# A two-layer graph attention kernel: a new order for the work ahead of the first period

## The chip, the cores and the metric

The kernel runs on one core of a Trainium2 chip. The metric is device time in microseconds (us). Before the change it was 3665.32 us, the median of three runs (3664.4 to 3667.73). The profiled execution took 3661.67 us and its trace spans 3659.8 us.

## What is computed

The input is 64 graphs of 256 nodes with 512 features, and a boolean 256 x 256 matrix for each graph. Two attention layers follow, each on the normalized and rectified input, each added to its input. Cut to what matters:

```python
# layer 0
h = max(layernorm(x), 0)
m = h @ map_w.T + map_b                       # 512 x 512
n = m / norm(m, per head of 64)               # "lengths", 8 heads
cos_adj = (n @ n.T > 0.1), where adj keeps it
q = m @ q_w.T + q_b;  k = m @ k_w.T + k_b     # 512 x 512 each
p = softmax(q @ k.T / 8, masked) * keep
sem = h @ gcn_map_w.T + gcn_map_b             # messages
out = relu((cos_adj * p) @ sem @ gcn_W.T / (sum(cos_adj * p) + 1))
x = x + out
# layer 1: q, k, v from 512 to 256 (4 heads), softmax under the adjacency, Wo
x = x + softmax(q1 @ k1.T / 8, masked) @ v1 @ Wo + bo
```

`gcn_W` is applied to the messages ahead of time: the kernel computes the folded weight `wc` from `gcn_map_w` and `gcn_W`, and the folded bias `bc`, once at the start.

## The kernel before

**Products.** Each 512 x 512 product on 256 nodes is done with seven half-size products in place of eight (`seven_products`, L260). For this each weight is held as seven blocks: four are loaded (`load_seven`, L72), and three are differences that VectorE computes with four subtractions of 128 x 512 (`finish_seven`, L85). The left factor, too, needs four sums, which GpSimd computes (`left_factors`, L250; the tile is `sh` for the normalized input and `sm` for the mapped one). A call of `seven_products` is a Python generator. At each `next` it issues one piece: p24 (two products into one bank, with biases added by ScalarE into u2 and u4), then z and p53 (u5), then a second product added into z, then a third one. Between the pieces VectorE reads z and writes a quarter of the result (L301) or the helper sum uup (L321). The next product into the same bank waits for that read. So TensorE, though it runs alone, hangs on VectorE at the last two pieces of each product.

**Order.** The whole schedule is written out by hand (`tc.manual_schedule()`). Every engine works through its instructions in the order in which the Python code issues them. An engine never overtakes: what stands behind a waiting instruction waits, too. Buffers are handed on in a ring[...], and waits follow from the data.

**Periods.** `period(i)` works on graph i in layer 0, on graph i - 1 in layer 1, and prepares graph i + 1 and graph i + 2. It is called 65 times and takes 56 us each time in the steady state. It begins with the score products `sc` (L401).

**The opening.** Ahead of the first period, the code at L712 to L761 has to bring graph 0 to where a period expects it, and graph 1 half way. It loads everything (L714 to L720), normalizes graph 0 (`normal`, then `normal_input`: transposes `p_t` on TensorE and `sh`), and prepares its edge mask. Then come, in this order:

- the differences of `wm` and the mapped input `mT` (`mapped`, tile `p_m`), with the fold of `wc` (`fold`, L120: 16 products, L127, evictions by ScalarE, L144) between its second and third piece,
- the differences of `wq`, the left factor `sm` and the squares, then the differences of `wk`,
- the first piece of the queries, the squared lengths (`norms`, L358, and `lengths`, L365), the folded bias (`fold_bias`, L131: VectorE spreads `gb` over `gbb`, TensorE multiplies, VectorE copies the bank into `bc`), and the differences of `wc`,
- the rest of queries and keys in turn,
- square root and reciprocal of the lengths (L749, L750) and their spread through DRAM (`spread`), edges and normalization of graph 1 (`normal(1)`), and a load of ScalarE's exp table ahead of its use (L755),
- the messages `p_s` of graph 0 (five pieces), and then graph 1's transposes and its `sh`.

**Loads.** Weights go through the SyncE queue one after the other (L82, L118, L184). The six small loads (`gt`, twice, `gb` and three biases, L44, L46, L95) go through ScalarE's queue. The biases are loaded as 128 x 4 single elements, and so make 512 packets of four bytes each. A completion semaphore is shared by every eighth of these loads, and the issue of a load waits until the load eight places before it has landed.

Of the kernel before, what the change touches and what calls it, by code (L numbers as in the profile page):

```python
# [8 lines left out]
F32 = mybir.dt.float32  # L9
# [20 lines left out]
class Weights:  # L30
# [4 lines left out]
    def __init__(self, nc, const, a):  # L35
        P, D, DH = 128, a["x"].shape[2], 64
        self.nc, self.const, self.a = nc, const, a
        self.ident = const.tile([P, P], F32, name="ident")
        make_identity(nc, self.ident)

        self.gt = const.tile([P, P], F32, name="gt")
        nc.vector.memset(self.gt, 0.0)
        for j in range(2):
            nc.scalar.dma_start(out=self.gt[j * DH:(j + 1) * DH, j * DH:(j + 1) * DH], in_=a["gcn_WT"])  # L44
        self.gb = const.tile([P, D // P], F32, name="gb")
        nc.scalar.dma_start(out=self.gb, in_=a["gcn_map_b"].rearrange("(c p) -> p c", p=P))  # L46
        self.ident_b = const.tile([P, P], BF16, name="ident_b")
        nc.vector.tensor_copy(self.ident_b, self.ident)
        self.below = const.tile([P, 1], F32, name="below")
        nc.vector.memset(self.below, -THRESHOLD)  # L50
        self.ones = const.tile([P, DH], F32, name="ones")
        nc.vector.memset(self.ones, 1.0)

        self.blk32 = const.tile([P, 32], F32, name="blk32")
        nc.vector.memset(self.blk32, 0.0)
        for j in range(2):
            nc.vector.memset(self.blk32[j * DH:(j + 1) * DH, j * 16:(j + 1) * 16], 1.0)

        self.two = const.tile([P, 2, 32], F32, name="two")
        nc.vector.memset(self.two, 0.0)  # L60
        for n in range(2):
            nc.vector.memset(self.two[:, n, n:n + 1], 1.0)
        self.wc = const.tile([P, 7, D // P // 2, D // 2], F32, name="wc")
        self.bc = const.tile([P, D], F32, name="bc")
# [4 lines left out]
        self.nc.sync.dma_start(out=t, in_=ap.rearrange("(c p) f -> p c f", p=128))  # L69
        return t  # L70

    def load_seven(self, keys, name):  # L72

        aps = [self.a[k] for k in (keys if isinstance(keys, tuple) else (keys, keys))]
        half = aps[0].shape[0] // 2
        t = self.const.tile([128, 7, half // 128, half], F32, name=name)
        for n, (i, j) in enumerate(self.BLOCKS):
            f = 0 if isinstance(keys, tuple) else j * half  # L80
            block = aps[j][i * half:(i + 1) * half, f:f + half]
            self.nc.sync.dma_start(out=t[:, n], in_=block.rearrange("(c p) f -> p c f", p=128))  # L82
        return t

    def finish_seven(self, t):  # L85
# [6 lines left out]
    def load_b(self, key, name):  # L92
        ap = self.a[key]
        t = self.const.tile([128, ap.shape[0] // 128], F32, name=name)
        self.nc.scalar.dma_start(out=t, in_=ap.rearrange("(c p) -> p c", p=128))  # L95
        return t

    def load_map(self):
        self.wm, self.bm = self.load_seven("map_wT", "wm"), self.load_b("map_b", "bm")

    def load_scores(self):
        self.wq, self.bq = self.load_seven("q_wT", "wq"), self.load_b("q_b", "bq")
# [14 lines left out]
        for k, t in enumerate(gws):  # L117
            self.nc.sync.dma_start(out=t, in_=gw[:, 2 * k:2 * k + 2, :])  # L118

    def fold(self, gws, bank, put):  # L120

        nc, P = self.nc, 128
        NKC = self.gb.shape[1]
        for c in range(NKC):
            p = bank(f"p_wc{c}", [P, NKC * P])
            for k in range(NKC):
                nc.tensor.matmul(p[:, k * P:(k + 1) * P], gws[k // 2][:, k % 2, c * P:(c + 1) * P], self.gt,  # L127
                                 start=True, stop=True)
            put(c, p)

    def fold_bias(self, gbb, bank):  # L131
        nc, P = self.nc, 128
        NKC = self.gb.shape[1]
        nc.vector.tensor_copy(gbb, self.gb[:, :, None].to_broadcast([P, NKC, P]))
        p = bank("p_bc", [P, NKC * P])
        for k in range(NKC):
            nc.tensor.matmul(p[:, k * P:(k + 1) * P], gbb[:, k, :], self.gt, start=True, stop=True)
        nc.vector.tensor_copy(self.bc, p)

    def put_seven(self, c, p):  # L140
        i, k = divmod(c, self.wc.shape[2])
# [6 lines left out]
def fast_path(ctx, tc, a, w, chk, out):  # L148
# [4 lines left out]
    nc = tc.nc  # L153
    x, adj = a["x"], a["adj"]
    B, S, D = x.shape
    P, DH = 128, 64
    H0, NKC = D // DH, D // P
# [6 lines left out]
    sb2 = ctx.enter_context(tc.tile_pool(name="sb2", bufs=2))  # L164
# [9 lines left out]
    def bank(name, shape=(P, 2, S), dtype=F32):  # L174
        return ring.tile(list(shape), dtype, tag="bank", name=name)
# [23 lines left out]
    def deviations(g):  # L199
        nc.scalar.activation(g.rs, g.rs, AF.Sqrt)  # L200
        nc.vector.reciprocal(g.rs, g.rs)
# [139 lines left out]
    def mapped(g):  # L341
        g.mT = sb1.tile([P, NKC, S], F32, tag="mT", name=f"mT{g.i}")
        return seven_products(g.left_h, w.wm, w.bm, g.mT, f"p_m{g.i}")
# [7 lines left out]
    def halved(g):  # L351
        g.left_m = left_factors(g.mT, "sm", g.i)
# [5 lines left out]
    def norms(g):  # L358

        p = bank(f"p_n{g.i}", [P, S])  # L360
        for c in range(NKC):
            nc.tensor.matmul(p[32 * c:32 * (c + 1), :], w.blk32, g.sq[:, c, :], start=True, stop=True)
        return p

    def lengths(g, p):  # L365
        g.rn = sb1.tile([P, S], F32, tag="rn", name=f"rn{g.i}")
        nc.vector.tensor_scalar_max(g.rn, p, COS_EPS * COS_EPS)
# [9 lines left out]
    def spread(g):  # L377

        g.nT = sb1.tile([P, NKC, S], F32, tag="nT", name=f"nT{g.i}")
        by_head(g.rn, 16, g.nT, f"rn{g.i}")  # L380
# [326 lines left out]
    def normal_input(g):  # L707
        g.hT = turned(g, f"0_{g.i}", "hT")
        g.left_h = left_factors(g.hT, "sh", g.i)

    with tc.manual_schedule():
        spare = small.tile([P, 2], F32, tag="spare", name="spare", bufs=1)  # L712
        nc.vector.memset(spare, 0.0)
        graphs = {0: load(0)}  # L714
        w.load_map()
        gws = [sb2.tile([P, 2, D], F32, tag="e", name=f"gw{k}", bufs=6) for k in range(2)]
        w.load_folded(gws)
        w.load_scores()
        graphs.update({n: load(n) for n in range(1, min(3, B))})
        w.load_rest()  # L720

        def normal(n):
            moments(graphs[n], f"0_{n}")
            deviations(graphs[n])
            normalized(graphs[n], f"0_{n}")

        g = graphs[0]
        normal(0)
        normal_input(g)
        edges(g)  # L730
        w.finish_seven(w.wm)
        m = mapped(g)
        next(m)
        next(m)
        w.fold(gws, bank, w.put_seven)
        next(m)
        w.finish_seven(w.wq)
        next(m)
        halved(g)
        squares(g)  # L740
        w.finish_seven(w.wk)
        q, k, s = queries(g), keys(g), messages(g)
        next(q)
        lengths(g, norms(g))
        w.fold_bias(sb2.tile([P, NKC, P], F32, tag="xn", name="gbb"), bank)
        w.finish_seven(w.wc)
        for step in (k, q, k, q, k, q, k):
            next(step)
        nc.scalar.activation(g.rn, g.rn, AF.Sqrt)  # L749
        nc.vector.reciprocal(g.rn, g.rn)  # L750
        spread(g)
        if B > 1:
            edges(graphs[1])
            normal(1)
        nc.scalar.activation(spare[:, 1:], spare[:, :1], AF.Exp)  # L755
        for _ in range(5):
            next(s)
        if B > 1:
            normal_input(graphs[1])
        if B > 2:  # L760
            moments(graphs[2], "0_2")  # L761
        for i in range(B + 1):
            period(i)
# [3 lines left out]
def general_path(ctx, tc, a, w, out):  # L767

    nc = tc.nc
    x, adj = a["x"], a["adj"]  # L770
    B, S, D = x.shape
    P, DH = 128, 64
    H0, NKC = D // DH, D // P
# [8 lines left out]
    wm = one.tile([P, NKC, D], F32, tag="gwm", name="gwm")  # L782
    nc.sync.dma_start(out=wm, in_=a["map_wT"].rearrange("(c p) f -> p c f", p=P))
    wc = one.tile([P, NKC, D], F32, tag="gwc", name="gwc")
    gws = [one.tile([P, 2, D], F32, tag=f"ggw{k}", name=f"ggw{k}") for k in range(2)]
# [20 lines left out]
    def bank(name, shape):  # L806
        return ps1.tile(shape, F32, tag="gbank", name=name)
# [71 lines left out]
                                     start=(k == 0), stop=(k == NT - 1))  # L879
        return av  # L880

    w.fold(gws, bank, lambda c, p: nc.vector.tensor_copy(wc[:, c, :], p))

    with tc.For_i(0, B) as b:
        xs = one.tile([P, NT, D], F32, tag="gxs", name="gxs")
# [11 lines left out]
        hT = norm_relu_T(xs, "0")  # L897
        mT = one.tile([P, NKC, S], F32, tag="gmT", name="gmT")
        nT = one.tile([P, NKC, S], F32, tag="gnT", name="gnT")
        for m in range(NKC):  # L900
            p = features_first(wm, hT, m, f"gp_m{m}")
# [3 lines left out]
        for t in range(NT):  # L905
            p = tokens_first(wc, hT, t, f"gp_s{t}")
            nc.vector.tensor_add(sem[:, t, :, :DH], p.rearrange("p (h d) -> p h d", d=DH),
                                 w.bc.rearrange("p (h d) -> p h d", d=DH))
        for m in range(NKC):
            sq = two.tile([P, S], F32, tag="gsq", name=f"gsq{m}")  # L910
            nc.gpsimd.tensor_mul(sq, mT[:, m, :], mT[:, m, :])
            p = bank(f"gp_n{m}", [P, S])
# [8 lines left out]
        for m in range(NKC):  # L921
            p = features_first(wq, mT, m, f"gp_q{m}")
            nc.scalar.activation(qT[:, m, :], p, AF.Identity, bias=w.bq[:, m:m + 1])
            p = features_first(wk, mT, m, f"gp_k{m}")
            nc.vector.tensor_scalar_add(kT[:, m, :], p, w.bk[:, m:m + 1])

        for t in range(NT):
            for g in range(H0 // 4):
                name = f"0_{t}_{g}"
# [21 lines left out]
        hT = norm_relu_T(xs, "1")  # L951
# [9 lines left out]
        for t in range(NT):  # L961
            p = tokens_first(w.wv1, hT, t, f"gp_v{t}")
            nc.scalar.copy(v[:, t, :, :DH], p.rearrange("p (h d) -> p h d", d=DH))
        for t in range(NT):
            name = f"1_{t}"
# [7 lines left out]
            p = bank(f"gp_oT{name}", [P, NIC, P])  # L973
# [4 lines left out]
            p = bank(f"gp_o{name}", [P, D])  # L978
# [83 lines left out]
```

## Time and profile before

| What | Value |
|---|---|
| Time, median of three | 3665.32 us |
| Span of the trace | 3659.8 us |
| TensorE (PE) busy | 3614.9 us, 99% |
| VectorE (DVE) busy | 2681.6 us, 73% |
| GpSimd (POOL) busy | 2226.7 us, 61% |
| ScalarE (ACT) busy | 1904.1 us, 52% |
| First transpose on TensorE | 7.90 us after the span's start |
| First score product `sc` | 55.73 us |
| One steady period | 56 us |

The times in the trace count from the span's start. A busy share is an average over the whole execution. The change touches only the first 56 us, which are 1.5% of the span, so the averages say nothing of it. What is needed is the order of instructions on each engine inside this stretch, who ends each idle time of TensorE, and the clock that TensorE was granted there. In a line of a stretch the columns are: from and to, length, busy time (and count of instructions) of PE, PEld (weight loads), DVE, ACT and POOL, granted clock, DMA share, GB/s. In a line of the timeline they are: start, time, engine, line, operation, output and input with shapes, count, and in brackets the idle time before it and what ended it. In a line of waits they are: who waited for whom, total us, number of times, longest.

### The profile page before, as it was taken

The numbers are of one execution on the slowest core, as the hardware profiler recorded it, in microseconds if no ns is written. First come the engines' busy times: TensorE is split into PE (matmuls) and PEld (weight loads), VectorE is DVE, ScalarE is ACT, GpSimd is POOL, SyncE is SP. The second block draws the span as 40 slices with busy tenths as digits, with TensorE's granted clock in tenths as the row PEclk, the third lists the DMA queues.
The fourth block names the chain that finished last, engine by engine and source line by source line (L and its number), as shares of the span: only waits on it lengthen the run. The fifth ranks groups of instructions, "written<-read, shape, count | busy, mean of one in ns | idle before, by whom it ended". The sixth has DMA issues, their size and how long they took to land.

```text
span 3659.8 us, 76416 instructions
## 1 busy us (share of the span) xinstructions
PE 3614.9 (99%) x29153; PEld 3088.7 (84%) x29153; DVE 2681.6 (73%) x5288; ACT 1904.1 (52%) x4480; POOL 2226.7 (61%) x2044
## 2 busy tenths in 40 slices
PE   7999999999999999999999999999999999999997
PEld 6888888888888888888888888888888888888885
DVE  6777777777777777777777777777777777777775
ACT  3455555555555555555555555555555555555543
POOL 3666566566665665666666656656666566566662
PEclk9999999999999999999999999999999999999999
DMA  3121211211211112112112111221121111211211
GB/s 110 46 57 45 56 45 53 60 44 54 58 45 55 51 50 58 44 55 60 43 53 57 47 55 45 53 60 44 53 58 45 55 51 50 58 44 55 60 30 35
DMA packets 361009, 191.73 MB, mean 52 GB/s; under 512 B 272449, under 2 KB 326977, under 8 KB 360641
## 3 DMA queue, kind: packets, MB, share of 16 engines
q1 hardware_dynamic: 358368, 186.76, 18.8%
q8 instruction: 233, 3.82, 0.4%
q14 instruction: 136, 1.11, 0.1%
q10 hardware_dynamic: 2272, 0.04, 0.0%
HBM read 94.67 MB, written 34.34 MB: 35 GB/s over the span
## 4 chain that ended last, share of the span: by engine, by line
PE 97%; DVE 1%; DMA 1%; POOL 0%; issue 0%; ACT 0%; SPq 0%; DVEq 0%; ACTq 0%; POOLq 0%
PE sc L401 9%; PE av L428 9%; PE p_m L276 6%; PE p_k L276 6%; PE p_q L276 6%; PE p_qk L276 6%; PE p_o L553 6%; PE p_v L520 6%; PE p_s L271 6%; PE co L438 5%; PE p_qk_z L276 5%; PE p_k_z L276 5%; PE p_q_z L276 5%; PE p_m_z L276 5%; PE p_s_z L271 4%; PE sm L481 2%
## 5 line engine op out<-in xcount | busy, mean ns | idle before, releaser
L421 POOL TENSOR_TENSOR d<-e 128x512 f32<-128x512 f32 x382 | 595.5, 1585 | 365.5 <-DVE e L417 364.2
L408 ACT ACTIVATE e<-sc 128x512 f32<-128x512 f32 x768 | 383.3, 648 | 382.7 <-PE sc L401 376.4
L465 POOL TENSOR_TENSOR d<-d,e 128x512 f32<-128x512 f32 x252 | 322.9, 1291 | 171.1 <-DVE e L463 171.1
L506 POOL TENSOR_TENSOR xs<-xs,o 128x512 f32<-128x512 f32 x128 | 188.4, 1495 | 341.6 <-DVE o L504 341.6
L254 POOL TENSOR_TENSOR sh<-hT 128x256 f32<-128x256 f32 x128 | 93.2, 728 | 492.6 <-ACT hT L217 315.7
L417 DVE TENSOR_TENSOR e<-e,mask 128x1024 f32<-128x1024 f32 x256 | 379.8, 1504 | 1.2 <-ACT e L408 1.2
L451 DVE SCALAR_TENSOR_TENSOR e<-co,e 128x256 f32<-128x256 f32 (+1 forms) x1024 | 288.0, 346 | 64.5 <-ACT up L448 35.4
L458 POOL TENSOR_TENSOR d<-d,e 128x512 f32<-128x512 f32 x252 | 312.4, 1270 | 0.0
L448 ACT ACTIVATE up<-co,below 128x128 bf16<-128x128 f32 x512 | 160.4, 364 | 185.9 <-PE co L438 180.4
L553 PE MATMUL p_o<-wo,own 128*128 128x512 f32 x512 | 233.7, 600 | 9.6 <-DVE own L548 9.6
L520 PE MATMUL p_v<-wv,hT 128*128 128x256 f32 x1024 | 242.2, 380 | 0.0
L428 PE MATMUL av<-e,sem 128*64 128x256 f32 x2048 | 232.4, 379 | 1.2 <-DVE e L463 1.2
L401 PE MATMUL sc<-qT,kT 64*128 64x256 f32 x2048 | 232.2, 377 | 0.0
L401 PEld LDWEIGHTS sc<-qT,kT 64*128 64x128 f32 x2048 | 198.6, 188 | 23.0 <-ACT hT L217 0.3
L491 DVE RECIPROCAL r<-rt 128x16 f32<-128x16 f32 x64 | 16.5, 258 | 269.1 <-PE rt L489 269.1
L428 PEld LDWEIGHTS av<-e,sem 128*64 128x64 f32 x2048 | 146.6, 137 | 76.3 <-DVE e L463 2.1
L520 PEld LDWEIGHTS p_v<-wv,hT 128*128 128x128 f32 x1024 | 185.0, 191 | 20.1 <-issue 0.3
L231 ACT ACTIVATE xn<-xs,shift,rs 128x512 f32<-128x512 f32 x124 | 100.5, 811 | 192.8 <-POOL d L458 190.3
L194 DVE BATCH_NORM_STATS2 st<-xs 128x6 f32<-128x512 f32 x256 | 173.9, 679 | 25.1 <-POOL xs L506 22.0
L463 DVE SCALAR_TENSOR_TENSOR e<-far,e 128x256 f32<-128x256 bf16 x256 | 189.8, 761 | 0.0
L438 PE MATMUL co<-nT 64*128 64x256 f32 (+1 forms) x2048 | 186.6, 332 | 2.8 <-ACT e L408 2.8
L438 PEld LDWEIGHTS co<-nT 64*128 64x128 f32 x2048 | 163.2, 189 | 21.9 <-ACT e L408 3.1
(198 smaller groups left out, 9279.3 us busy)
## 6 DMA issues: line engine op xcount, KB each, us to landing
xs<-in_x_dram SPq DMA_DIRECT2D x64, 512.0 KB
nT<-by_rn SPq DMA_DIRECT2D x128, 256.0 KB
out_dram<-xs SPq DMA_DIRECT2D x63, 512.0 KB
own<-by_rz SPq DMA_DIRECT2D x128, 128.0 KB
ad<-in_adj_dram SPq DMA_DIRECT2D x64, 64.0 KB
far<-up SPq DMA_TRANSPOSE x256
turn<-flat SPq DMA_TRANSPOSE x248
mask<-adb SPq DMA_TRANSPOSE x128
```

Source lines behind the costliest of these rows:

```text
L271: nc.tensor.matmul(region, src[:, c, :], wt[:, block, c, :], start=p not in opened, stop=True, skip_group_check=True)
L276: nc.tensor.matmul(region[:, f, :], wt[:, block, c, f * P:(f + 1) * P], src[:, c, :], start=p not in opened, stop=True, skip_group_check=True)
L401: nc.tensor.matmul(ps[s][:, j, :], rows[h, c, j * P:(j + 1) * P], cols[h, c, :], start=True, stop=True)
L408: nc.scalar.activation(e[:, s, :], p.rearrange("p j q -> p (j q)"), AF.Exp, scale=SCALE)
L417: nc.vector.tensor_mul(e, e, m)
L421: nc.gpsimd.tensor_add(d, e[:, :, :S], e[:, :, S:])
L428: nc.tensor.matmul(av[s * DH:(s + 1) * DH, n, :], vs[:, j, (h0 + s) * DH:(h0 + s + 1) * DH], q[:, s, j * S:(j + 1) * S], start=(j == 0), s ...
L438: nc.tensor.matmul(ps[s][:, j, j * P:], g.nT[h, c, j * P:(j + 1) * P], g.nT[h, c, j * P:], start=(j == 0), stop=True, skip_group_check=True)
L458: nc.gpsimd.tensor_add(g.d[c], g.d[c], g.e[c][:, :, :S])
L465: nc.gpsimd.tensor_add(g.d[c], g.d[c], g.e[c][:, :, S:])
L520: nc.tensor.matmul(g.p_v[:, t, :], g.h1T[:, c, t * P:(t + 1) * P], w.wv1[:, c, :], start=(c == 0), stop=(c == NKC - 1))
L553: nc.tensor.matmul(p, b.avs1[:, c, t * P:(t + 1) * P], w.wo1[:, c, :], start=(c == 0), stop=(c == NIC - 1))
```

## The change

The opening is put in another order, so that VectorE's work for the weights stands where VectorE was idle, and its work for the lengths and for graph 1 stands beside TensorE's queries and keys. In detail:

- The differences of `wq` follow the first piece of the mapped input, those of `wk` the second, both ahead of the sums that read z.
- The fold of `wc` is split: columns 0 and 1 after the first piece of the mapped input, columns 2 and 3 after the third.
- The spread of the bias, `gbb`, is an operation of its own, right behind the differences of `wm`. The product `p_bc` follows the mapped input directly, and ScalarE, not VectorE, copies it to `bc`.
- The differences of `wc` precede the queries.
- The lengths follow the first pieces of both queries and keys. Square root, reciprocal and spread, and graph 1's edges and normalization, come right behind it and after the queries' second piece, instead of behind all queries and keys. The exp table is loaded there as well.
- Graph 1's transposes precede the last piece of the messages; its `sh` follows it.
- The blocks of `wm` alternate between the SyncE and the ScalarE queue. The six small loads move to GpSimd's queue.

No computation is added or left out.

```diff
-            nc.scalar.dma_start(out=self.gt[j * DH:(j + 1) * DH, j * DH:(j + 1) * DH], in_=a["gcn_WT"])
+            nc.gpsimd.dma_start(out=self.gt[j * DH:(j + 1) * DH, j * DH:(j + 1) * DH], in_=a["gcn_WT"])
...
-        nc.scalar.dma_start(out=self.gb, in_=a["gcn_map_b"].rearrange("(c p) -> p c", p=P))
+        nc.gpsimd.dma_start(out=self.gb, in_=a["gcn_map_b"].rearrange("(c p) -> p c", p=P))
...
-            self.nc.sync.dma_start(out=t[:, n], in_=block.rearrange("(c p) f -> p c f", p=128))
+            queue = (self.nc.sync, self.nc.scalar)[n % queues]
+            queue.dma_start(out=t[:, n], in_=block.rearrange("(c p) f -> p c f", p=128))
...
-        self.nc.scalar.dma_start(out=t, in_=ap.rearrange("(c p) -> p c", p=128))
+        self.nc.gpsimd.dma_start(out=t, in_=ap.rearrange("(c p) -> p c", p=128))
...
-        self.wm, self.bm = self.load_seven("map_wT", "wm"), self.load_b("map_b", "bm")
+        self.wm, self.bm = self.load_seven("map_wT", "wm", 2), self.load_b("map_b", "bm")
...
-    def fold(self, gws, bank, put):
+    def fold(self, gws, bank, put, cs):
...
-        for c in range(NKC):
+        for c in cs:
...
+    def spread_bias(self, gbb):
+        self.nc.vector.tensor_copy(gbb, self.gb[:, :, None].to_broadcast([128, self.gb.shape[1], 128]))
+
     def fold_bias(self, gbb, bank):
...
-        nc.vector.tensor_copy(gbb, self.gb[:, :, None].to_broadcast([P, NKC, P]))
...
-        nc.vector.tensor_copy(self.bc, p)
+        nc.scalar.copy(self.bc, p)
...
         w.finish_seven(w.wm)
+        gbb = sb2.tile([P, NKC, P], F32, tag="xn", name="gbb")
+        w.spread_bias(gbb)
+
         m = mapped(g)
         next(m)
+        w.fold(gws, bank, w.put_seven, (0, 1))
+        w.finish_seven(w.wq)
         next(m)
-        w.fold(gws, bank, w.put_seven)
+        w.finish_seven(w.wk)
         next(m)
-        w.finish_seven(w.wq)
+        w.fold(gws, bank, w.put_seven, (2, 3))
         next(m)
         halved(g)
         squares(g)
-        w.finish_seven(w.wk)
+        w.fold_bias(gbb, bank)
+        w.finish_seven(w.wc)
         q, k, s = queries(g), keys(g), messages(g)
         next(q)
+        next(k)
         lengths(g, norms(g))
-        w.fold_bias(sb2.tile([P, NKC, P], F32, tag="xn", name="gbb"), bank)
-        w.finish_seven(w.wc)
-        for step in (k, q, k, q, k, q, k):
-            next(step)
         nc.scalar.activation(g.rn, g.rn, AF.Sqrt)
         nc.vector.reciprocal(g.rn, g.rn)
         spread(g)
+        next(q)
         if B > 1:
             edges(graphs[1])
             normal(1)
         nc.scalar.activation(spare[:, 1:], spare[:, :1], AF.Exp)
-        for _ in range(5):
-            next(s)
+        for step in (k, q, k, q, k, s, s, s, s):
+            next(step)
         if B > 1:
-            normal_input(graphs[1])
+            graphs[1].hT = turned(graphs[1], "0_1", "hT")
+        next(s)
+        if B > 1:
+            graphs[1].left_h = left_factors(graphs[1].hT, "sh", 1)
```

More of the change, by code (lines that the diff above doesn't have):

```diff
@@ L70, in load_w, with load_seven @@
         return t
-    def load_seven(self, keys, name):
+    def load_seven(self, keys, name, queues=1):
         aps = [self.a[k] for k in (keys if isinstance(keys, tuple) else (keys, keys))]
@@ L880, in mix @@
         return av
-    w.fold(gws, bank, lambda c, p: nc.vector.tensor_copy(wc[:, c, :], p))
+    w.fold(gws, bank, lambda c, p: nc.vector.tensor_copy(wc[:, c, :], p), range(NKC))
     with tc.For_i(0, B) as b:
```

## The prediction

> **What bounds the kernel now.** I read the page first, then stage totals, then TensorE's waits, then VectorE's order, then the granted clock.
>
> ```profile
> span 3659.8 us, 76416 instructions
> ...
> PE 3614.9 (99%) x29153; PEld 3088.7 (84%) x29153; DVE 2681.6 (73%) x5288; ACT 1904.1 (52%) x4480; POOL 2226.7 (61%) x2044
> ...
> PE   7999999999999999999999999999999999999997
> ```
>
> TensorE is busy in all slices but the first and the last. The edit touches only what comes before the first period, so stages tell what there is to gain:
>
> ```profile
> 7.90:55.73 47.83, 38.21 (x261) 33.92 (x262) 28.87 (x56) 12.72 (x35) 9.80 (x12) 0.94 0.54 163
> ...
> 110.00:166.00 56.00, 56.00 (x455) 47.95 (x455) 41.38 (x83) 29.81 (x70) 34.86 (x33) 1.00 0.19 52
> ```
>
> Columns: stretch, length, busy PE, PEld, DVE, ACT, POOL, granted clock, DMA share, GB/s. A steady period has no TensorE idle. The opening, from TensorE's first transpose (7.90) to its first score product `sc` (55.73), has 47.83 - 38.21 = 9.62 us idle, at a mean clock of 0.94. Who ends that idle time:
>
> ```profile
> PE p_bc L137 <- DVE gbb L134: 3.1, 1, 3.1
> PE p_s_z L271 <- DVE sem L301: 2.4, 1, 2.4
> PE p_q L276 <- DVE mT L301: 1.5, 1, 1.5
> PE p_m L276 <- DVE wm L90: 1.4, 1, 1.4
> PE p_m_z L276 <- DVE uup_m L321: 0.6, 1, 0.6
> PE p_s_z L271 <- DVE uup_s L321: 0.5, 1, 0.5
> ```
>
> Every gap is a wait for VectorE, whose order of work is at fault, not its speed:
>
> ```profile
> 21.57 0.42 DVE L321 TENSOR_TENSOR uup_m<-p_m_z,u5p_m 128x256 f32<-128x256 f32 x1 [5.83 <-PE p_m_z L276]
> ...
> 28.79 1.09 DVE L90 TENSOR_TENSOR wk<-wk 128x512 f32<-128x512 f32 x1
> 29.81 0.41 DVE L367 TENSOR_SCALAR rn<-p_n 128x256 f32<-128x256 f32 x1
> 30.14 0.61 DVE L134 COPY gbb<-gb 128x512 f32<-128x512 f32 x1
> ```
>
> VectorE idles 5.83 us, then does the wq and wk differences while TensorE waits. Last, the clock:
>
> ```profile
> 47.00:49.00 2.00, 0.15 (x1) 0.00 (x0) 1.69 (x6) 1.69 (x3) 0.00 (x0) 1.00 0.16 24
> ...
> 50.00:51.00 1.00, 1.00 (x4) 0.67 (x2) 0.00 (x0) 0.00 (x0) 0.00 (x0) 0.50 1.07 210
> ...
> 56.00:57.00 1.00, 1.00 (x8) 0.86 (x10) 0.93 (x3) 0.43 (x1) 0.49 (x1) 0.71 0.00 0
> ```
>
> After the 2.42 us gap the clock is 0.50 until some 56.5. Two groups of `p_s_z` take 1.93 and 2.08 us there against 1.03 at 72.66, and eight transposes 1.91 against 1.04 for eight at 90.50: 0.90 + 1.05 + 0.87 = 2.8 us. So the gap costs more than its length.
>
> **What the Trainium skill says.** "TensorE: Matmul & The Clock Gate", Part 1, says that an idle window of about 3.4 us halves the clock and that the windows run freely. The trace agrees in kind: halved after 2.42 us of idle at 47.15 and again after 2.23 us at 95.11, but not after 3.15 us at 27.75, so where the gap falls matters. "SBUF — State Buffer", Who interferes with whom, says that a VectorE operation with two SBUF inputs contends with GpSimd. It does: a 128x512 difference takes 0.69 us alone, 1.10 beside GpSimd's sums (`wk`, L88 to L90). "DMA: Bandwidth & Descriptors", Issuing engines are not separate DMA queues, says that a second issuing engine saves issue time only; and its SWDGE section, that GpSimd writes its own descriptors, with some 1 us to the first byte. No run here shows a GpSimd load.
>
> **The change part by part.** Times are after the edit unless marked. A product of seven runs as p24, z, p53, z(s2), z(s3); before each z(s..) TensorE waits until VectorE has read z for the last time.
>
> *Loads.* The wm blocks leave at once on two queues; before, the fourth issue ended at 6.66 because it waited for the gt load (4.41 us in the chain of waits). Against this, two blocks (0.5 MB) now run beside graph 0's input. Delay of that input: none if they fill idle DMA time (share 0.81 in the first 10 us), 0.52 MB / 361 GB/s = 1.45 us if they go wholly ahead. I take 0.6: first transpose 8.5, xn ready at 8.8. wm's differences then no longer wait 1.01 us for a load: 0.69 + 0.22 (ident_b, now second) + 2 x 0.69 + 1.10 = 3.4, end 12.2, against 13.03. TensorE's cold start ends at the same place, so its 1.4 us wait nearly goes.
>
> *Six small loads on GpSimd.* Price unknown: lower bound the skill's 1 us each, done by about 7.3; upper bound by the nearest row, queue q10, 0.1% x 16 x 3659.8 / 2272 packets = 26 ns each as rounded, 11.6 ns with 1.5% of the first 110 us: 2048 four-byte packets x 11.6 = 24 us. I take 1 to 2.5 us each[...]. GpSimd's queue holds sh behind them (10.55 before, 11.1 now); p53 needs its last sum only at about 16.8 and sh takes 2.9 to 3.7 us, so up to some 12 us for the six is hidden. gt is due at 13.2, bm at 13.2; both fit.
>
> *Middle of the mapping.* TensorE: p_m second half 12.25 to 13.15; half the fold (3.58 / 2 = 1.79) to 14.95 (gw had landed at 12.77); z 0.89, p53 1.79 to 17.65. VectorE: gbb 0.61 (hidden: wq has not landed), wq's four from about 15.0 to 17.8, mT 18.2; so z(s2) waits 0.6: 18.25 to 19.2. Second half of the fold to 21.0. wk landed at 18.75 in the chain; I keep that: four x 0.69 to 21.5, uup 21.9. So the last z waits 0.95: 21.95 to 22.95, and mT is whole at 23.8 instead of 25.89. Gain 2.1. GpSimd is idle here, hence 0.69.
>
> *After mT.* p_bc follows at once (gbb is long ready), 0.93 to 23.9; p_q 1.8, p_k 1.79, p_n 0.55, q z 0.89: q53 begins at 28.9 instead of 34.54. Gain so far 5.6; the 3.15 and 1.52 us gaps are in it. sm on GpSimd needs 4.5 us as before (beside wc's differences, 0.69 + 3 x 1.10), ready at 28.3, just in time. bc on ScalarE (0.65) is hidden: nobody needs it before the messages.
>
> *Lengths and graph 1's norm under queries and keys.* VectorE after wc (27.8): rn 28.4, sqrt on ScalarE 28.85, reciprocal 1.74 to 30.6, q's first sum 31.0, moments 1.9, sqrt and reciprocal 0.5, xn 1.0 to 34.5, k's first sum 34.9. Behind it waits k's z(s2), which TensorE reaches at 34.3: a new gap of 0.65. The exp table load (1.28) on ScalarE ends at 34.5 ahead of u5 for the keys, needed at 35.8: hidden.
>
> *Messages.* VectorE now holds only their own sums, so the 2.42 us gap goes, and with it the halved clock; graph 1's transposes fill the 0.5 us gap. From q53 to `sc`: 4.47 + 0.89 + 0.65 + 2.73 (three z) + 4.32 (p_s, z, p_s53) + 0.88 + 0.95 + 0.88 = 15.8, with starts 16.1, against 21.19 before. `sc` starts at 45.0 instead of 55.73: **10.7 us gained**. sh for graph 1 comes after the last product, done some 4 us after `sc` begins, and is needed 7.7 us after (63.43 - 55.73). moments(2) ends 1 to 2 us later against `sc`; the masks had 1.15 us of wait, and PE there a queue of scores. Hidden. From `sc` on everything moves as a block: 3665.3 - 10.7 = 3654.6.
>
> **Rivals.** (1) *Timed runs lack the halved clock*, as windows run freely: the gain is 10.7 - 2.8 = 7.9, 3657.4. For: no halving after the 3.15 us gap. Against: half clock three times near the end too, so gaps of this size do hit. (2) *Loads late*: GpSimd's issues at 11.6 ns a packet, 24 us from 1.3, hold sh until 25.3, done 28.2; p53's half 0.9, z 0.95, fold 1.8, z 0.95 and the last sums 0.85 bring mT whole at 33.7 instead of 23.8. Of 10.7 remain 0.8: 3664.5. At 18 us in all mT is whole at 27.7 and 6.8 remain: 3658.5. For: the price is unseen. Against: some 12 us of room. (3) *Slower*: descriptors at twice that, 48 us: sh done at 52.2, mT whole at 57.7, 31.8 after before's 25.89; 10.7 - 2.1 = 8.6 is won later, so 3665.3 + 23.2 = 3688.5. Only the unseen price speaks for it.
>
> **Chances.** Main case 0.62 (3654.6, within 3651 and 3658: input delay 0 to 1.45, wk up to 0.6 us earlier, and one more or less halved window, 3.4 us at half speed = 1.7), rival 1 0.14, rival 2 0.19, rival 3 0.05. Low end 3650.0: mildest bounds (1.2 us) and two halved windows fewer (3.4). High end 3661.5: the middle of rival 2's two sizes. Faster needs under 3658.0: most of the main case, two thirds of rival 1, and a third of rival 2: 0.75; same 0.20; slower 0.05.
>
> **What would show it.** `sc` starting near 45; `p_bc` and `p_s_z` with no wait; clock 1.00 from 12 us to `sc`; TensorE idle in the opening about 2.5 us; wk's differences at 0.69; a steady period still 56.0 us. Wrong if sh starts after 13 (GpSimd's loads), if the first transpose is later than 9.3 (input crowded), or if VectorE waits on wq or wk past 19.

## The result, and the profile after

After takes **3650.43 us** (median of six runs, 3649.96 to 3652.85), before 3664.75 us (six runs, 3663.11 to 3667.73): ratio **0.9961, 95% interval 0.9948 to 0.9974**. That is 14.3 us gained, where 10.7 were forecast.

The page of after, its busy times and TensorE's row of slices, looks as before: only the first slice differs at all.

```profile
span 3651.0 us, 76421 instructions
...
PE 3613.9 (99%) x29153; PEld 3088.9 (85%) x29153; DVE 2680.1 (73%) x5287; ACT 1902.7 (52%) x4481; POOL 2229.8 (61%) x2050
...
PE   8999999999999999999999999999999999999997
```

The work is the same (TensorE 3613.9 against 3614.9 us busy), and a stage shows what the slices can't. Stage totals of after, first transpose to first `sc`, and a steady period:

```profile
8.30:44.41 36.11, 35.27 (x261) 32.81 (x261) 26.77 (x50) 13.55 (x37) 9.52 (x12) 1.00 0.71 205
97.00:153.00 56.00, 56.00 (x456) 47.95 (x455) 41.46 (x82) 29.79 (x70) 34.97 (x32) 1.00 0.17 47
```

The opening has 36.11 - 35.27 = 0.84 us of TensorE idle, in place of 9.62, at a mean clock of 1.00, in place of 0.94. The period is 56.00 us still. What is left of TensorE's waits from 7 to 46 us, after the wait for the first input:

```profile
PE p_m L279 <- DVE wm L91: 0.4, 1, 0.4
PE p_k_z L279 <- DVE kT L304: 0.2, 1, 0.2
PE p_m_z L279 <- DVE uup_m L324: 0.2, 1, 0.2
```

The waits for `gbb`, for `mT` ahead of the queries, and for graph 0's sums are gone. VectorE's order of time in after shows by what:

```profile
15.35 0.69 DVE L88 TENSOR_TENSOR wq<-wq 128x512 f32<-128x512 f32 x1 [2.06 <-DMA wq<-in_L_gnn_q_w_dram]
...
18.14 0.42 DVE L304 TENSOR_TENSOR mT<-p_m_z,u2p_m 128x256 f32<-128x256 f32 x1
18.47 0.68 DVE L88 TENSOR_TENSOR wk<-wk 128x512 f32<-128x512 f32 x1
...
21.25 0.42 DVE L324 TENSOR_TENSOR uup_m<-p_m_z,u5p_m 128x256 f32<-128x256 f32 x1
```

The bracket is VectorE's own idle time and its cause. It waits for data now (the load of `wq`), and both sets of differences are done before the mapping's last sums of `mT`. In before the differences of `wq` stood directly ahead of these last sums:

```profile
24.53 0.69 DVE L90 TENSOR_TENSOR wq<-wq 128x512 f32<-128x512 f32 x1
25.14 0.42 DVE L301 TENSOR_TENSOR mT<-p_m_z,u5p_m 128x256 f32<-128x256 f32 x1
```

Those of `wk` stood behind them and ahead of `gbb`. TensorE waited for `mT` and for `gbb` in turn. At the end of the opening, TensorE's order of time in after has the one wait that the prediction put there, and `sc`:

```profile
34.61 1.16 PE L279 MATMUL p_k_z<-sm,wk 128*128 128x128 f32 x8 [0.25 <-DVE kT L304]
...
44.41 3.72 PE L404 MATMUL sc<-qT,kT 64*128 64x256 f32 x32
```

So `sc` begins 55.73 - 44.41 = 11.3 us earlier in the two profiled executions. This is not yet 14.3.

### The profile page after: what moved, and what is told of

The parts are those of the page before. It is cut to its first block, busy times and chain, and to the rows that moved or that the text cites. A ratio compares the mean times of both kernels' runs of the same rounds, so it can differ in the third digit from the quotient of the medians.

```text
span 3651.0 us, 76421 instructions
## 1 busy us (share of the span) xinstructions
PE 3613.9 (99%) x29153; PEld 3088.9 (85%) x29153; DVE 2680.1 (73%) x5287; ACT 1902.7 (52%) x4481; POOL 2229.8 (61%) x2050
## 4 chain that ended last, share of the span: by engine, by line
PE 97%; DVE 1%; DMA 1%; POOL 0%; issue 0%; ACT 0%; SPq 0%; ACTq 0%; DVEq 0%; POOLq 0%
PE sc L404 9%; PE av L431 9%; PE p_q L279 7%; PE p_m L279 7%; PE p_qk L279 6%; PE p_k L279 6%; PE p_o L556 6%; PE p_v L523 6%; PE p_s L274 6%; PE co L441 5%; PE p_qk_z L279 5%; PE p_m_z L279 5%; PE p_q_z L279 5%; PE p_k_z L279 5%; PE p_s_z L274 4%; PE sm L484 2%
## 5 line engine op out<-in xcount | busy, mean ns | idle before, releaser
L556 PEld LDWEIGHTS p_o<-wo,own 128*128 128x128 f32 x512 | 94.5, 195 | 105.7 <-issue 102.4
```

The costliest lines, as they stand in the source:

```text
L556: nc.tensor.matmul(p, b.avs1[:, c, t * P:(t + 1) * P], w.wo1[:, c, :], start=(c == 0), stop=(c == NIC - 1))
```

## The experiments

Two theories. **Order**: the gain is the idle time taken out, and the move of everything behind it. **Clock**: much of it is TensorE running at half speed after these waits and in its cold start, which no longer happens. A smaller question was which part of the edit does it.

| Kernel | Time, us (range, runs) | Ratio to before (95%) | `sc` begins, us | span less `sc` |
|---|---|---|---|---|
| before, profiled execution | 3661.67 | | 55.73 | 3604.1 |
| before again | 3664.78 (3661.93-3666.50, 13) | 1.0 (0.9992-1.0009) | 61.01 | 3603.1 |
| late gap filled | 3663.14 (3659.82-3665.89, 13) | 0.9995 (0.9986-1.0003) | 56.84 | 3603.8 |
| middle gap filled | 3664.77 (3659.26-3667.65, 13) | 0.9998 (0.9990-1.0007) | 57.97 | 3604.8 |
| all gaps filled | 3660.06 (3657.96-3662.96, 21) | 0.9987 (0.9981-0.9994) | 54.15 | 3602.0 |
| loads only | 3662.46 (3660.96-3664.47, 13) | 0.9994 (0.9986-1.0003) | 57.04 | 3603.6 |
| after, profiled execution | 3652.85 | | 44.41 | 3606.6 |
| order only | 3651.10 (3650.22-3652.05, 5) | 0.9963 (0.9949-0.9976) | 46.87 | 3602.4 |
| after, one queue for wm | 3650.55 (3650.05-3650.90, 5) | 0.9963 (0.9950-0.9977) | 45.56 | 3602.9 |
| late part undone | 3651.61 (3651.15-3652.39, 5) | 0.9965 (0.9951-0.9978) | 46.57 | 3602.5 |
| middle part undone | 3654.68 (3652.88-3656.06, 7) | 0.9971 (0.9959-0.9982) | 49.52 | 3604.5 |
| after, later gaps filled | 3644.74 (3644.38-3645.65, 5) | 0.9946 (0.9933-0.9960) | 44.17 | 3598.3 |
| the same, 28 products ahead | 3646.02 (3645.38-3646.57, 5) | 0.9951 (0.9938-0.9965) | 45.52 | 3598.5 |
| the same, 18 products ahead | 3644.46 (3644.28-3647.09, 5) | 0.9949 (0.9936-0.9963) | 44.32 | 3598.2 |

The last two columns are of one profiled execution each. Each ratio is taken against runs of before beside that kernel, whose median was between 3663.56 and 3665.11 us. So medians of two kernels that were measured at different times can't be told apart when they differ by about 1 us. What follows `sc` takes 3602 to 3607 us in every kernel without later fillers. The openings differ by more than that.

**Before, once more.** No edit.

> The kernel before once more, for the span and the mean granted clock of each run. Order theory (the gain is TensorE's waits for VectorE, some 8 us of idle, and what is over is the half clock that the profiled run shows): all runs at the same clock as the profiled one, 0.996, spans within 1 us of one another. Clock theory (half-clock windows fall differently in each run, and in timed runs the openings of before catch more of them than its profile shows): runs near 3665 us have a lower mean clock than a run near 3662; 3.4 us more at half clock are 1.7 us more time and 0.0005 less mean clock.

The median repeats. The runs spread over 4.6 us, where the order theory expected 1, and the slowest has a mean clock of 0.995, the fastest 0.997. Of all 99 executions of before in these experiments, 30 have 0.997 and a median of 3663.54 us, and 67 have 0.996 and 3664.78 us. This is the direction that the clock theory expected; the clock is recorded to three digits, so its size can't be checked. And this execution has another opening than the profile that the prediction was read from. TensorE's order of time:

```profile
14.30 2.05 PE L276 MATMUL p_m<-hT,wm 128*128 128x128 f32 x8 [2.66 <-DVE wm L90]
...
20.52 3.74 PE L127 MATMUL p_wc<-gt,gw 128*128 128x128 f32 x32
...
34.59 2.05 PE L137 MATMUL p_bc<-gt,gbb 128*128 128x128 f32 x8 [3.15 <-DVE gbb L134]
36.44 3.62 PE L276 MATMUL p_k<-mT,wk 128*128 128x128 f32 x16
```

`wm` was ready later (a wait of 2.66, not 1.4 us); half speed went on until about 19.7 us (worked out from the durations), so the fold began at 20.52, not 16.83; and after the 3.15 us wait `p_bc` took 2.05 us (1.06 in after), and `p_k` 3.62 (1.95 in after). `sc` began at 61.01, 5.3 us later than in the first profile. So the opening of one execution doesn't stand for the others.

**Gaps of before filled, one at a time.** Products that nobody reads stand in front of the waiting one, so that TensorE is busy; no real work moves.

```diff
+    def filler(n, name):
+        p = bank(f"fill{name}", [P, 2 * P])
+        for _ in range(n):
+            nc.tensor.matmul(p, w.ident, w.wm[:, 0, 0, :], start=True, stop=True)
...
             next(s)
+            if n == 2:
+                filler(3, "s")            # late gap
...
         lengths(g, norms(g))
+        filler(5, "n")                    # middle gap (the other kernel)
```

> The kernel before with three products of 128x256 into a spare bank (results unused) in TensorE's queue where it waits 2.42 us for VectorE in the messages. No wait is shortened. Clock theory: the clock stays at 1.00 from 47 us on, p_s_z take 1.0 us and not 1.93 and 2.08, the eight transposes 1.0, sc starts about 2.8 us earlier, near 52.9; time 2.5 to 3.4 us lower, about 3661.6. Order theory with no role for the clock: no change, or 0 to 1.3 us longer.

> The kernel before with five such unused products (2.1 us) in TensorE's 3.15 us wait for gbb. In the profile of before the clock is not halved after this wait. If the timed runs of before look like its profile: no change. If in timed runs this wait does halve the clock: 1.7 to 3.4 us less, about 3662.

With the late gap filled, what followed it ran at full speed in the profiled run (`p_s_z` 1.13 us at 53.25), and the median is 1.4 us below that of before beside it (3664.54); the interval of the ratio still holds 1. The middle filler covers 2.43 of 3.15 us: no half speed there (`p_k` 1.95 us at 34.76), but half speed followed the late gap from about 53 us on, and the median did not move. The low runs did: the lowest of the 33 runs of before beside them took 3662.45 us, and 5 of 13 runs with the late gap filled, and 4 of 13 with the middle one, were faster. One filler helps some executions and not others, so filling one gap alone doesn't settle the question.

**All gaps of before filled.** Both fillers (8 in the middle), and two more: 28 products of 128x128 ahead of the first transpose, 4 in the wait for `wm`.

```diff
+        warm = bank("warm", [P, P])
+        for _ in range(28):
+            nc.tensor.matmul(warm, w.ident, w.ident, start=True, stop=True)
         normal_input(g)
...
         product("24", p24[:, 0], 1, a12)
...
+        if name == "p_m0":
+            filler(4, "m")
```

> The order of before with TensorE kept busy in its gaps by products whose result nobody reads: 28 of 128x128 ahead of the first transpose, 4 of 128x256 in the wait for wm's differences, 8 in the 3.15 us wait for gbb and 3 in the 2.42 us wait for graph 0's sums. No wait of real work is shortened. If the gain is mostly the order (idle time taken out) and the half clock is the smaller share, this wins only that share: about 2.6 us of the cold start (fold from 17.9 instead of 20.5) and 1.2 late, so some 3661 (3659 to 3662.5) with sc near 57, and after stays 10 us ahead. If the waits cost mainly through the clock, this comes near after: 3655 or less. If the cold start is made up for later (its time hidden behind the 3.15 us wait, which ends when VectorE gets there), it wins only the 1.2 to 1.6 of the late filler: 3663.3.

TensorE's order of time shows the opening at full speed, and the waits that stay:

```profile
9.52 1.04 PE L216 MATMUL p_t<-ident,xn 128*128 128x128 f32 x8
...
26.34 1.16 PE L276 MATMUL p_q<-mT,wq 128*128 128x128 f32 x8 [1.52 <-DVE mT L301]
...
54.15 3.73 PE L403 MATMUL sc<-qT,kT 64*128 64x256 f32 x32
```

3660.06 against 3665.01 us: **half speed alone is about 5.0 us of before's time** (2.2 to 7.0 by the interval of the ratio). The time is in the range that the order theory gave, and 9.6 us above after. In the two profiles `sc` is 9.7 us apart (54.15 and 44.41). This part is what the new order takes out where half speed plays no role, so for the most part TensorE's idle time. The fillers weren't free: the 8 in the middle ran past the time when `gbb` was ready, as `p_bc` follows them without a wait. The 28 products ran past the first transpose's due time, but `p_m`'s second half was bound by `wm` anyway (13.91 us).

**Order without the loads, loads without the order.**

```diff
# order only: after, with these four as before
-            nc.gpsimd.dma_start(out=self.gt[...
+            nc.scalar.dma_start(out=self.gt[...
...                                   # gb and load_b alike
-        self.wm, self.bm = self.load_seven("map_wT", "wm", 2), ...
+        self.wm, self.bm = self.load_seven("map_wT", "wm"), ...
# loads only: before, with the same lines changed the other way
```

> The new order with all loads on their old queues (small ones on ScalarE's, wm on SyncE's alone). Cold-start theory (in most runs of before the late wm differences leave TensorE idle for 1.5 to 2.8 us right after its start, so that it stays at half clock until about 19 us; the early wm of the new queues prevents this, and that is what the timed gain has over the 10.7 us of the forecast): TensorE still at half clock in the fold's first half and p53, 2.5 to 4 us longer than the changed kernel, about 3653.5. Order theory (loads give only the shorter wait for wm, 1 us, mostly hidden by wq's landing): 3650.4 to 3651.4.

> The old order with only the queues of the loads changed. Cold-start theory: second half of p_m near 12.6, full clock from about 13.8, the fold begins 3 us earlier than in most runs of before; 3 to 4 us less, about 3661. Order theory: the input lands 0.4 us later and wm's wait is 1 us shorter, 3664.

The order alone has nearly all of the gain (3651.10). Its trace starts worse than that of after:

```profile
13.26 2.05 PE L279 MATMUL p_m<-hT,wm 128*128 128x128 f32 x8 [1.63 <-DVE wm L91]
15.10 3.62 PE L128 MATMUL p_wc<-gt,gw 128*128 128x128 f32 x16
```

Half speed lasted to 19.4 us (the half fold took 3.62 us in place of 1.95), and `sc` came 2.5 us later than in after's profile. The 0.7 us between the medians is within the spread of the runs. So the trace has the half speed that the cold-start theory expected, and the median (3651.10) hasn't the 3653.5 us that went with it; why is open. The loads alone, in the old order, shorten the cold start (the wait for `wm` is 0.22 us, the fold begins at 16.50), but the old waits halve the clock behind them:

```profile
30.57 2.04 PE L137 MATMUL p_bc<-gt,gbb 128*128 128x128 f32 x8 [3.15 <-DVE gbb L134]
...
50.75 2.07 PE L271 MATMUL p_s_z<-wc,sh 128*128 128x256 f32 x4 [2.42 <-DVE sem L301]
```

2.65 us below the before beside it (3665.11), with 1 still in the interval.

**Which half of the load change?** After, with `wm` on one queue and the small loads on GpSimd.

```diff
-        self.wm, self.bm = self.load_seven("map_wT", "wm", 2), ...
+        self.wm, self.bm = self.load_seven("map_wT", "wm"), ...
```

> After with wm's four blocks on one queue again, the six small loads still on GpSimd: tells which half of the load change moves wm. If the small loads ahead of wm held it up (the fourth issue ended at 6.7 us in before), wm's differences start at 9.1 to 9.5 and end by 12.6, p_m waits 0.4, and the time is that of after, 3650.4. If the second queue is what brings wm early, the differences end at about 13.2, p_m waits 1.6 and the cold clock lasts to about 19, as in order_only: 3651.1 or a little less.

The four issues of `wm` ended at 3.79 us instead of 6.7, and its differences still began at 9.40 (9.42 in order only). So the held-up issue did not set when `wm` arrived. With two queues they began at 9.14: the second queue brought 0.26 us. This agrees with "DMA: Bandwidth & Descriptors", Issuing engines are not separate DMA queues, by which starting loads from several engines saves only the time to start them. They ended at 12.43 instead of 13.1, mostly because GpSimd's `sh` came later here (10.96 us), so three differences instead of two ran uncontended at 0.69 us. `sc` moves by 1.2 us in the traces, the median by 0.1: not to be told apart.

**The middle and the late part undone in after.**

```diff
# middle: fold whole, differences of wq and wk behind the mapping's last pieces
-        w.fold(gws, bank, w.put_seven, (0, 1))
-        w.finish_seven(w.wq)
         next(m)
-        w.finish_seven(w.wk)
+        w.fold(gws, bank, w.put_seven, (0, 1, 2, 3))
         next(m)
-        w.fold(gws, bank, w.put_seven, (2, 3))
+        w.finish_seven(w.wq)
         next(m)
         halved(g)
         squares(g)
+        w.finish_seven(w.wk)
# late: square root, reciprocal, spread, edges(graphs[1]), normal(1)
#       again behind all pieces of queries and keys
```

> The changed kernel with the fold in one piece and the differences of wq and wk back where they were (behind the third and the fourth piece of the mapped input); gbb's early spread, wc's differences ahead of the queries, and all that follows stay. The 1.5 us wait for the last sums of mT returns, and VectorE has 2.9 to 4 us of wk's differences ahead of wc's and of the lengths, so q's and k's z wait some 3 us; in all 3 to 5 us more, 3654.5. Rival: TensorE has queries and keys to do meanwhile, only the 1.5 us return: 3652.

> The changed kernel with square root, reciprocal and spread of the lengths and graph 1's edges and normalization put back behind all queries and keys, the transposes of graph 1 left where they are. Both theories: the 2.4 us wait of p_s_z for VectorE returns. With the half clock that follows it in before: 5 to 5.5 us more, 3655.7. If the clock stays full: 2.2 us more (2.4 less the 0.25 us wait of p_k_z that goes), 3652.6.

With the middle part undone TensorE waits for `wk`'s differences, and the clock halves behind it:

```profile
29.67 1.38 PE L279 MATMUL p_k<-mT,wk 128*128 128x128 f32 x8 [2.28 <-DVE wk L91]
...
31.99 2.04 PE L279 MATMUL p_q_z<-mT,wq 128*128 128x128 f32 x8
```

It is the keys' first piece that waits, and not the later pieces as expected. This costs 4.3 us in the median, 5.1 at `sc`. With the late part undone the 2.42 us wait is back to the hundredth, but this time without half speed behind it:

```profile
43.77 1.13 PE L274 MATMUL p_s_z<-wc,sh 128*128 128x256 f32 x4 [2.42 <-DVE sem L304]
```

`sc` moves by 2.2 us, the median by 1.2, which is hardly to be told apart. The two and the loads (0.7) sum to 6.1 of 14.3 us. What none of these kernels undoes is the early `gbb` and `p_bc`, which took the largest wait (3.15 us) out, and the early differences of `wc`; these were not tried alone, so their share is not shown. Parts undone one by one also need not sum to the whole, since each wait also decides whether the clock halves.

**After, with its later gaps filled.** The same waits for VectorE stand later in after, untouched by the edit: in period 0 ahead of layer 1's transposes, and ahead of `p_o` in periods 63 and 64.

```diff
+        if i >= B - 1:
+            filler(3 if i < B else 13, f"o{i}")
         if b:
             for t in range(NT):
                 result(b, t)
...
+        if i == 0:
+            filler(3, "t0")
         if g:
             g.h1T = turned(
```

> The changed kernel with unused products in TensorE's remaining waits: three ahead of graph 0's layer-1 transposes in period 0 (2.24 us wait), three ahead of the output products of period 63 (2.43 us) and thirteen ahead of those of period 64 (7.0 us). No wait is shortened. Clock theory: no half clock after these three, p_t 1.0 us instead of 1.93, each p_o group 3.4 to 4.3 us instead of 5 to 6.7; 1.7 us less in period 0 and 1 to 2.5 us less at each p_o, together 3.5 to 5.5 us: about 3646. Order theory with no role for the clock: 3650.4, no change.

TensorE's order of time around one of these, first in after, then with the filler:

```profile
3605.63 6.68 PE L556 MATMUL p_o<-wo,own 128*128 128x512 f32 x8 [2.43 <-DVE own L551]
```

```profile
3602.99 3.67 PE L556 MATMUL p_o<-wo,own 128*128 128x512 f32 x8 [1.23 <-DVE own L551]
```

6.68 us became 3.67, the `p_o` of period 64 went from 6.18 to 3.67, and period 0's transposes from 1.93 to 1.08. **3644.74 us: 5.7 us below after**, with no overlap of the runs, for 19 products thrown away.

**And its cold start.** The kernel above with 28, then 18, products ahead of the first transpose and 4 in the wait for `wm` (the diff of "all gaps filled").

> After with the fillers of a_fill (period 0, periods 63 and 64), and 28 products of 128x128 ahead of the first transpose plus 4 of 128x256 in the wait for wm. If the cold clock still costs in the opening, the eight transposes take 1.0 instead of 1.9 us and the second half of p_m 0.9 instead of 1.8: sc 0.9 to 2 us earlier and 3642.7 to 3643.8, against 3644.7 for a_fill. If VectorE's order alone sets the opening (wm's differences end at 12.4 either way), no more than 0.3 us: 3644.4. If the dummy products run on past the first transpose's due time, up to 0.5 us slower.

> As a_best, with 18 products of 128x128 ahead of the first transpose in place of 28. In a_best the 28 ran from 2.71 to 10.88 us, as 56 passes: some 6 a microsecond cold until 6, 9 to 7, then 12. So 18 (36 passes) end at about 7.7, ahead of the first transpose at 8.2. Theory that the cold clock sets the opening of after: first transpose near 8.2, the eight in 1.0, sc 0.5 to 1 us earlier than in a_fill (44.2), and 3643.7 to 3644.3. Rival, VectorE's differences of wm set it (they end at 12.4 either way, p_m's second half begins there): sc within 0.3 of 44.2 and 3644.5 to 3645.

The 28 were mis-sized: I had priced them like transposes, but a 128x128 product stands as two records in the trace (56 in all), so they ended at 10.88 us, about 2.6 late, and cost 1.3 us. With 18, TensorE's order of time is

```profile
9.39 1.04 PE L219 MATMUL p_t<-ident,xn 128*128 128x128 f32 x8
...
13.40 1.05 PE L279 MATMUL p_m<-hT,wm 128*128 128x128 f32 x8
```

They still ended 1.2 us late (9.39 against 8.2), yet `sc` came only 0.15 us after that of the kernel without them, and the medians (3644.46 and 3644.74) can't be told apart. `p_m`'s second half began 1.0 us later (13.40 against 12.40) at no cost, because VectorE's differences of `wq` wait for their load, until 15.25 us here and 15.11 without the products, and what follows up to `mT` hangs on them. So the warm start brought nothing here. One that ended in time was not tried.

## Why the prediction was right, and where it was too small

The 3650.43 us measured lie just below the main case (3651 to 3658) and above the low end of 3650.0, which the prediction kept for its mildest bounds and two halved windows fewer. The table compares its steps with the trace.

| Step of the prediction | Forecast | Profile of after |
|---|---|---|
| first transpose, input delayed by 0.6 us | 8.5 | 8.30 |
| `wm`'s differences end | 12.2 | 12.43 |
| cold start ends | about 12.2 | about 14.0 |
| six small loads on GpSimd | 1 to 2.5 us each | 0.55 to 0.94 each |
| `wq`'s differences from | 15.0 | 15.35 |
| `wk`'s differences end | 21.5 | 21.33 |
| waits before z(s2) and z(s3) of the mapping | 0.6 and 0.95 | none and 0.17 |
| `mT` whole | 23.8 | 23.7 |
| `q53` begins | 28.9 | 28.84 |
| wait before the keys' z(s2) | 0.65, until 34.9 | 0.25, until 34.61 |
| TensorE idle in the opening | about 2.5 | 0.84 |
| `sc` begins | 45.0 | 44.41 |
| steady period | 56.0 | 56.00 |

**The order of events held, step by step.** VectorE's times were within 0.4 us; the differences ran in its idle time; the bias, the lengths and graph 1's norm were hidden where the prediction hid them; and no new wait took the old ones' place. The small waits came out smaller mostly because TensorE itself was later: cold for 1.8 us longer, it reached z(s2) when VectorE was done. That is a wait exchanged for slow work, and `mT` was on time either way. After with its later gaps filled shows the other side: `p_m`'s second half took 1.13 us there, not 1.81, TensorE waited 0.36 us before z(s2), and the last sum of `mT` began at 23.02, not 23.26. That `sc` came out within 0.6 us of the forecast is thus in part luck: the forecast had too much idle time and too little slow work.

**Rivals 2 and 3 fall with one view.** GpSimd's order of time in after:

```profile
1.32 0.94 POOL L46 DMA_DIRECT2D gb<-in_L_gnn_gcn_map_b_dram  x1 [0.36 <-issue]
...
2.60 1.09 POOL L44 DMA_DIRECT2D gt<-in_L_gnn_gcn_W_dram  x2
3.68 0.78 POOL L96 DMA_DIRECT2D bm<-in_L_gnn_map_b_dram  x1
...
10.96 0.92 POOL L257 TENSOR_TENSOR sh<-hT 128x256 f32<-128x256 f32 x1 [5.00 <-ACT hT L220]
```

A load of 512 four-byte elements holds GpSimd for 0.78 us, that is 1.5 ns an element. Both of my bounds were prices of something else: the upper one, 11.6 ns, of packets in another queue, the lower one, 1 us a load, of the way to the first byte, and the issues took less than that. GpSimd had been idle for 5.00 us when `sh` began, and it waited for `hT`, not for loads.

**The step that was too small is the clock.** The prediction booked 2.8 us of half speed, read from one trace, and took its `sc` at 55.73 as before's start. But that execution (3661.67 us) was 3.1 us below before's median, and below each of before's six runs; the one taken again has `sc` at 61.01. Other executions of before can have a longer cold start, and half speed behind the 3.15 us wait as well (in two of the four traces, of before and its variants, that have this wait unfilled): 5.0 us in the median, by the kernel with all gaps filled. The stage of before again, first transpose to `sc`, has the idle time to go with it:

```profile
7.80:61.01 53.21, 42.36 (x260) 38.67 (x261) 29.10 (x54) 12.52 (x35) 10.34 (x12) 0.90 0.48 146
```

53.21 - 42.36 = 10.85 us idle, less the 0.84 left in after, less 0.5 for the later first transpose (8.30 against 7.80): 9.5 us, close to the 9.6 between all gaps filled and after. With the 5.0 this makes 14.5 us, against 14.3 measured. The sum is an account and no experiment of its own, and that it fits so well is in part luck. The 5.0 holds a cold start that after still has, and is a difference of medians. In this one execution the slow work was 42.36 - 35.27 = 7.1 us more than in after, and `sc` came 16.6 us later. The 14.3 lie between the 11.3 and the 16.6 of the two profiled executions.

**Rival 1 had the sign wrong.** It said that timed runs lack the half speed in the profile; by the 5.0 us in the median (with the cold start), and as the profiled execution was faster than all six of them, they have more of it. "TensorE: Matmul & The Clock Gate", Part 1, warns that the number of cold products changes from run to run with the phase of the windows. The traces agree that it changes: one execution of before was at full speed when the second half of `p_m` began at 13.18 us, the other not before about 19.7. They don't show that the phase alone does it, since the wait for `wm` differed too (1.43 and 2.66 us). I used that page to explain a window I saw and not to doubt a window I didn't see.

**From `sc` on, a block:** right within what the windows allow. The span less `sc` was 3604.1 us in before's profile and 3606.6 in after's, which was the longest of its six runs; the other five lie 2.1 us and more below it. So of `sc`'s 11.3 us only 3661.67 - 3652.85 = 8.8 show between the two profiled executions. The 2.5 us that are missing lie in the last two periods, behind waits that the edit doesn't touch. The `p_o` of period 63 took 6.68 us in after, and in before

```profile
3617.27 5.09 PE L553 MATMUL p_o<-wo,own 128*128 128x512 f32 x8 [2.43 <-DVE own L548]
```

after the same wait; that of period 64 took 6.18 and 5.40. From the first of them to the end of the span it is 45.4 us in after and 42.5 in before, and 0.3 us go the other way earlier. So this is half speed again, more in one execution than in the other, and no cost of the new order.

## What to carry to other kernels

In the opening of a long kernel, list the waits of the busiest engine by who ends them: where all of them name one engine that itself idles for data earlier, moving its preparatory work into that idle time takes them out, and the gain can be worked out from the trace step by step. Each such wait can cost more than its length, as what comes after may run at half speed; take that share from several executions, since a single profile showed 2.8 us where 5.0 were to be had. Where a wait can't be removed, a few products without use ahead of it gave 5.7 us here, but at the start of the kernel, where VectorE's loads and differences set the pace, they gave nothing.

## What the runs showed of the hardware that was not expected

- The same wait halves the clock in one run and not in another: 2.42 us did in before and in loads only, and did not in late part undone; 3.15 us did not in before's first profile, and did in before again and in loads only. The two waits of 1.13 us (late gap filled, all gaps filled) were not followed by it.
- The cold start is not in the clock column. In after's stage from 8.30 us the granted clock reads 1.00, while eight transposes took 1.94 us, and 1.04 later. It is read from durations.
- TensorE kept busy from 1.37 us on, with products only, was still slow until about 5 us (3 products a microsecond, later 6). Kept busy from 2.71 us on, it was slow until about 6.5 us in one execution (28 products) and about 8.2 in another (18 products).
- The issues of `wm` ended 2.9 us earlier, and its differences began no earlier (9.40 and 9.42 us).
